# One store and one load per transpose, tiled products of two batches together, and a scheduler that models DMA: a four-layer graph network on one core

## Chip, cores and metric

The kernel runs on one core of one Trainium2 chip, in float32. The metric is device time in microseconds (us), the median of several executions. Engines are named as in the profile: PE (TensorE), DVE (VectorE), ACT (ScalarE), POOL (GpSimd), SP (SyncE, which issues DMAs). "A trip" is the way of a block through DRAM: store, load, transpose.

## The reference, cut to what matters

128 batches of 128 nodes with 512 features pass through four graph layers; each is `x = layernorm(x + layer(x, adj))`.

```python
# layer 0: H = sum_k Xk @ Wk[k] + bk[k], Xk = transition @ Xk (k = 0..2), transition from exp(leaky_relu(..)) * adj
# layer 1: two hypergraph convolutions, 512 -> 1024 -> 512, with relu and a layer norm between them
# layer 2: out = A @ x @ w, A from exp(lrelu(8 * tanh((s_i + s_j) / 8))) * adj
# layer 3: attention, 8 heads of 64; mask = adj + adj
q, k, v = proj(Wq, bq), proj(Wk, bk), proj(Wv, bv)
scores = einsum('bhqd,bhkd->bhqk', q, k) * SCALE * mask
ctx = einsum('bhqk,bhkd->bhqd', softmax(scores), v)
x = layernorm(x + ctx @ Wo.T + bo)
```

## The kernel before

Batches go in 64 pairs. The large products run as Strassen products (seven block products on PE, gathered from PSUM banks by DVE, ACT and POOL). All instructions of the whole program are first put in a list; a small simulation in the kernel file (`Plan.order`) then decides the order on every engine and which buffer each tile gets. **So an edit of one constant can move every instruction of the program.**

The left operands of the products have to be transposed. The kernel has DVE's transpose turn blocks of 32 x 32 (Q in the code) and leaves the moving of the blocks to a trip through DRAM: each of the four groups of 32 partitions is stored by its own DMA, one DMA loads the whole, DVE turns the blocks.

```python
def through_dram(src, name):
    _, nj, _, nw = src.shape
    d = scratch(name, 4, Q, 4, nj, nw)                    # Q = 32
    for j in range(nj):
        with plan.together():
            for m in range(4):
                sp.dma_start(part(d, lambda t, m=m, j=j: t.rearrange("k r m j w -> m j r k w")[m, j], j),
                             src[m * Q:(m + 1) * Q, j])
    def load():
        t = four()...                                     # cut: or sq() for the small ones
        sp.dma_start(t, part(d, lambda t: t.rearrange("k r m j w -> (k r) (m j w)"), 0, nj))
        return t
    return load

def turned(dst, t):
    ve.transpose(dst.rearrange("p q (m r) -> p m q r", r=Q), t.rearrange("p (m q a) -> p m q a", m=4, a=Q))

# layer 3, scores (cut; the product with v has the same form, one group per batch)
for b in range(U):                                        # U = 2 batches of a pair
    ps = [bank(), bank()]
    with plan.together(.6):
        for i in range(C):
            for r2 in range(2):
                pe.matmul(ps[r2][:, i * P:(i + 1) * P], qT[r2 * HD:(r2 + 1) * HD, b, i],
                          kT[r2 * HD:(r2 + 1) * HD, b, i], start=True, stop=True)
    # cut: DVE takes the banks into S, softmax, through_dram(S)
```

`four` is a tile of 128 x 1024 numbers (17 of them exist), `sq` one of 128 x 256, `bank` a PSUM bank (eight). The scheduler's estimate of a DMA was 60 ns of SP and 4500 ns until it has landed.

## Time and profile before

| | before |
|---|---|
| time, median of 3 runs | 5815.66 us (5813.88 to 5820.15) |
| busy: PE / DVE / POOL / ACT | 97% / 62% / 50% / 34% |
| transposes 128 x 1024 on DVE | 384, 1229 ns each |
| DMAs to store h, S and x3 for a trip | 4 per plane of 128 partitions |

The prediction below shows the busy shares, the windows and the timeline. Two more views matter later. First four lines of the page: groups of instructions (columns: busy us, mean ns of one, then idle time just before them and what ended it) and DMA issues (count, KB each, median us from issue to landing).

```profile
L307 PE MATMUL bank<-w,four 128*128 128x256 f32 (+1 forms) x14336 | 4044.3, 436 | 42.0 <-DVE four L307 31.1
...
L307 DVE STREAM_TRANSPOSE four<-four 128x1024 f32<-128x1024 f32 x384 | 467.5, 1229 | 75.3 <-DMA four<-x 31.0
...
h<-four SPq DMA_DIRECT2D x512, 128.0 KB, 2.4
four<-h SPq DMA_DIRECT2D x128, 512.0 KB, 3.9
```

And the largest wait of PE (who waits, for whom; then us in all, number of waits, longest):

```profile
PE bank L307 <- DVE four L307: 86.8, 63, 18.3
```

PE waits for DVE 63 times in the whole run. One of these waits, of 18.3 us, is that at the tail.

### The profile page before, as it was taken

Reading aid. Unit: us, or ns where it says so; the run is one execution under the profiler, and the core shown is the slowest. Engines: PE = TensorE matmul, PEld = TensorE weight load, DVE = VectorE, ACT = ScalarE, POOL = GpSimd, SP = SyncE. Lnnn points to the kernel's source line nnn. Section 1 sums busy time; section 2 is a strip of 40 time slices with the busy share of each in tenths; the row PEclk is TensorE's granted clock in tenths of the full one; section 3 lists DMA queues with packets and bytes.
Section 4 is the critical chain, followed back from the end, with each engine's and each line's share of the span. In section 5 each row is a group of like instructions: output and inputs, shape, how many; then the busy total and the mean of one; then the engine's idle time right before and its main releaser. Section 6 shows DMA issues by size and latency. Waiting matters only on the chain.

```text
span 5816.9 us, 87982 instructions
## 1 busy us (share of the span) xinstructions
PE 5665.4 (97%) x29077; PEld 4174.5 (72%) x29077; DVE 3591.1 (62%) x7654; ACT 1956.3 (34%) x5065; POOL 2895.7 (50%) x4553
## 2 busy tenths in 40 slices
PE   7999999999999999999999999999999999999997
PEld 4555555555666666666666688888888888888886
DVE  5656656665556555555555556666666666666664
ACT  1322222222333333333333333333333333333332
POOL 2333333332656666666666545555555555555553
PEclk9999999999999999999999999999999999999998
DMA  5433333332433344433333434444444444444443
GB/s 142 115 90 95 90 88 95 93 86 85 119 113 114 113 117 121 119 113 114 113 117 113 122 96 123 117 120 124 128 122 123 116 120 124 126 123 117 118 123 90
DMA packets 731128, 653.96 MB, mean 112 GB/s; under 512 B 270760, under 2 KB 584112, under 8 KB 730672
## 3 DMA queue, kind: packets, MB, share of 16 engines
q1 hardware_dynamic: 730672, 648.32, 38.7%
q8 instruction: 232, 3.80, 0.3%
q14 instruction: 224, 1.84, 0.1%
HBM read 362.81 MB, written 285.21 MB: 111 GB/s over the span
## 4 chain that ended last, share of the span: by engine, by line
PE 79%; DMA 8%; POOL 5%; DVE 3%; SPq 3%; issue 2%; ACT 1%; DVEq 0%; POOLq 0%; ACTq 0%
PE bank L307 79%; POOL four L307 3%; SPq L307 3%; DVE four L307 2%; DMA four<-x 2%; DMA four<-x1d 2%; POOL col L307 1%; ACT four L307 1%; DMA h<-four 1%; DMA four<-h 1%; DMA sq<-in_adj_dram 1%; DVE col L307 1%; DMA four<-in_x_dram 0%; DVE junk L307 0%; DMA four<-in_L_gnn_w_dram 0%
## 5 line engine op out<-in xcount | busy, mean ns | idle before, releaser
L307 PE MATMUL bank<-w,four 128*128 128x256 f32 (+1 forms) x14336 | 4044.3, 436 | 42.0 <-DVE four L307 31.1
L307 PEld LDWEIGHTS bank<-w,four 128*128 128x128 f32 x14336 | 2675.2, 191 | 1223.5 <-issue 789.7
L307 DVE TENSOR_TENSOR four<-bank,four 128x256 f32<-128x256 f32 (+1 forms) x1920 | 922.2, 483 | 1360.3 <-PE bank L307 1256.9
L307 ACT COPY four<-bank 128x256 f32<-128x256 f32 (+1 forms) x1280 | 571.4, 453 | 2173.2 <-PE bank L307 2160.3
L307 POOL TENSOR_TENSOR four<-four 128x256 f32<-128x256 f32 (+1 forms) x704 | 593.3, 855 | 1135.7 <-DVE col L307 620.4
L307 PE MATMUL bank<-four,w 128*128 128x128 f32 x7168 | 828.3, 276 | 31.6 <-DVE four L307 30.7
L307 PEld LDWEIGHTS bank<-four,w 128*128 128x128 f32 x7168 | 816.3, 193 | 47.2 <-issue 29.0
L307 POOL TENSOR_TENSOR four<-four,four 128x256 f32<-128x256 f32 (+1 forms) x832 | 708.5, 855 | 15.9 <-issue 1.4
L307 ACT ACTIVATE four<-four,col,col 128x512 f32<-128x512 f32 (+1 forms) x640 | 568.7, 897 | 438.1 <-POOL col L307 427.6
L307 POOL TENSOR_SCALAR col<-col 128x1 f32<-128x1 f32 (+1 forms) x704 | 213.3, 306 | 980.0 <-DVE col L307 946.5
L307 ACT ACTIVATE four<-four,col 128x128 f32<-128x128 f32 x1024 | 396.4, 393 | 679.1 <-DVE col L307 679.1
L307 DVE BATCH_NORM_STATS2 col<-four 128x6 f32<-128x512 f32 x768 | 523.2, 687 | 139.0 <-ACT four L307 128.0
L307 DVE STREAM_TRANSPOSE four<-four 128x1024 f32<-128x1024 f32 x384 | 467.5, 1229 | 75.3 <-DMA four<-x 31.0
L307 POOL TENSOR_TENSOR col<-col,neghalf 128x1 f32<-128x1 f32 x640 | 385.6, 605 | 22.9
L307 PE MATMUL bank<-four,sq 128*128 128x512 f32 x768 | 383.5, 594 | 10.2 <-ACT four L307 6.5
L307 PE MATMUL bank<-four,four 64*128 64x128 f32 (+1 forms) x4096 | 290.7, 284 | 21.2 <-DVE four L307 21.2
L307 PEld LDWEIGHTS bank<-four,four 64*128 64x128 f32 (+1 forms) x4096 | 235.4, 163 | 105.6 <-issue 43.7
L307 ACT ACTIVATE four<-four 128x512 f32<-128x512 f32 (+1 forms) x272 | 172.9, 636 | 347.9 <-DVE four L307 312.0
L307 POOL TENSOR_TENSOR four<-four,col 128x1024 f32<-128x1024 f32 x128 | 242.2, 1913 | 59.6 <-DVE col L307 59.6
L307 PEld LDWEIGHTS bank<-sq,four 128*128 128x128 f32 x2048 | 245.2, 193 | 29.3 <-issue 28.9
L307 PE MATMUL bank<-sq,four 128*128 128x128 f32 x2048 | 250.9, 276 | 0.0
L307 DVE SCALAR_TENSOR_TENSOR four<-bank,col,four 128x512 f32<-128x512 f32 x320 | 229.4, 730 | 22.3 <-PE bank L307 19.3
(77 smaller groups left out, 3419.5 us busy)
## 6 DMA issues: line engine op xcount, KB each, us to landing
h<-four SPq DMA_DIRECT2D x512, 128.0 KB, 2.4
four<-h SPq DMA_DIRECT2D x128, 512.0 KB, 3.9
S<-four SPq DMA_DIRECT2D x512, 128.0 KB, 2.5
four<-S SPq DMA_DIRECT2D x128, 512.0 KB, 4.3
four<-in_x_dram SPq DMA_DIRECT2D x64, 512.0 KB, 3.6
four<-in_x_dram SPq DMA_DIRECT2D x512, 64.0 KB, 2.1
x1d<-four SPq DMA_DIRECT2D x64, 512.0 KB, 2.9
four<-x1d SPq DMA_DIRECT2D x64, 512.0 KB, 5.5
```

Source lines behind the costliest of these rows:

```text
L307: call(*map(real, args), **{n: real(a) for n, a in kw.items()})
```

## The change

Its intent: fewer DMA issues, shorter trips, half as many changes of PE's tiling, and an order made with truer DMA times. The core of the diff (cut: bookkeeping of `run`, `parts` and DRAM tiles, deadlines, wider use of `ac.mul`):

```diff
-WHEN0 = (-3.0, -1.8, -.4, 0, .7)
+WHEN0 = (-1.5, -1.2, -.4, 0, .7)
-WHEN2 = (-2.4, -2.0, -1.35, -1.0, -.6, 0, .35, .7, .72, 1.2, 1.3, 1.31, 1.6)
-LAG1, LAG2 = 1, 1
+WHEN2 = (-2.4, -2.0, -1.35, -1.0, -.6, 0, .35, .7, 1.25, 1.6)
+LAG1, LAG2 = 1, 0.5
+RAMP = 0, 0, .2, 6
@@ LATENCY, row of SP
-           (4500, 4500, 4500, 4500, 4500))
+           (1400, 1400, 1400, 1400, 1400))
+ISSUE, BEGIN = 450, 1000
+EARLY = -0.5
@@ order: a DMA's transfer goes through one pipe; loads are gated by how far PE has come
+                if e == SP and ops[k][3][0] > reached and not ops[k][4]:
+                    continue
+            if o[7]:
+                end = pipe = max(pipe, t + BEGIN) + o[7]
@@ through_dram
-        d = scratch(name, 4, Q, 4, nj, nw)
+        d = scratch(name, 4, P, nj, nw)
         for j in range(nj):
-            with plan.together():
-                for m in range(4):
-                    sp.dma_start(... "k r m j w -> m j r k w" ..., src[m * Q:(m + 1) * Q, j])
+            sp.dma_start(part(d, lambda t, j=j: t.rearrange("k p j w -> j p k w")[j], j), src[:, j], run=nw)
-            sp.dma_start(t, ... "k r m j w -> (k r) (m j w)" ...)
+            sp.dma_start(t, ... "k (r m) j w -> (k r) (m j w)", m=4 ..., run=4 * nj * nw)
@@ turned
-    def turned(dst, t):
-        ve.transpose(dst.rearrange("p q (m r) -> p m q r", r=Q), t.rearrange("p (m q a) -> p m q a", m=4, a=Q))
+    def turned(dst, t, chunks=1):
+        src = t.rearrange("p (n a c) -> p n c a", a=Q, c=chunks) if chunks > 1 else t.rearrange(
+            "p (m q a) -> p m q a", m=4, a=Q)
+        ve.transpose(dst.rearrange("p q (r m) -> p m q r", r=Q), src)
@@ layer 3: one group for both batches (same for the product with v)
-        for b in range(U):
-            ps = [bank(), bank()]
-            with plan.together(.6):
+        ps = [[bank(), bank()] for _ in range(U)]
+        with plan.together(.65):
+            for b in range(U):
@@ prepare0: weights of the first products first, issued by ACT
+        load_blocks(WT["2"], wk0[2][:, :h], wk0[2][:, h:], True, ac.dma_start)
+        load_blocks(WT["10"], wk0[1], wk0[0], True, ac.dma_start)
```

`WHEN0` to `WHEN2` and `LAG1`, `LAG2` give every stage of a pair its place in the list, counted in pairs (the "key" of the prediction).

The price of the single store stands in `turned`. A row of the batch used to be numbered `32 m + r` (m the group of 32 partitions), so that what DVE wrote for one block was a run of 32 neighbouring numbers. Now it is `4 r + m`: neighbours in a block are written **four numbers, 16 bytes, apart**. For x, h and x3 the features are renumbered too, so that the transposes also read at 16 bytes (`c = 4`) or 32 bytes (`c = 8`, h).

> **What bounds the kernel now.** I read the page first (busy shares, the 40 slices), then a table of eight windows, then the waits of TensorE, then the timeline at the start, in steady layer 2/3 and at the tail.
>
> ```profile
> PE 5665.4 (97%) x29077; PEld 4174.5 (72%) x29077; DVE 3591.1 (62%) x7654; ACT 1956.3 (34%) x5065; POOL 2895.7 (50%) x4553
> ```
>
> TensorE (PE) is the bound: 97% busy, the next engine 62%. DMA engines are 38.7% busy. So only two things can move the time: PE instructions that become cheaper, and the 151 us in which PE has nothing to do. The windows (columns: length, then busy us and count of PE, PEld, DVE, ACT, POOL; granted clock, DMA share, GB/s) say where that idle time is:
>
> ```profile
> 0.00:60.00 60.00, 20.52 (x49) 12.19 (x50) 31.70 (x72) 6.04 (x15) 8.41 (x20) 0.91 0.83 217
> 290.00:1450.00 1160.00, 1160.00 (x3519) 657.23 (x3518) 696.85 (x1588) 284.99 (x685) 368.89 (x634) 1.00 0.32 91
> 1450.00:1750.00 300.00, 278.59 (x1065) 182.43 (x1064) 170.76 (x355) 112.81 (x191) 178.31 (x299) 0.98 0.39 116
> 1750.00:3200.00 1450.00, 1432.42 (x5465) 952.83 (x5465) 846.57 (x1728) 534.57 (x862) 894.72 (x1462) 1.00 0.40 115
> 3200.00:3500.00 300.00, 277.53 (x1603) 226.43 (x1602) 175.48 (x361) 97.86 (x256) 145.62 (x223) 0.97 0.37 108
> 3500.00:5670.00 2170.00, 2156.89 (x15870) 1915.66 (x15869) 1446.49 (x3081) 809.55 (x2740) 1163.09 (x1712) 1.00 0.42 122
> 5670.00:5817.00 147.00, 113.19 (x789) 96.67 (x787) 72.22 (x141) 44.26 (x161) 56.59 (x82) 0.88 0.31 92
> ```
>
> Idle PE: 39 us at the start, 21 and 22 at the two changes of layer, 34 at the tail; steady layer 0 has none, steady layer 1 18, steady layer 2/3 13. The starts of successive PE records show more than "busy" does, because a PE end is modelled. In clean stretches the step is 216 ns after a 256-column instruction, 429.5 after 512, 111.5 after 128, 109 after one with the identity, and on average 57 inside a tiled group (64 rows or 64 columns). Counts by these steps give a **floor of 5525 us**. The other 292 us are the pool from which any gain comes.
>
> Part of it is not idle at all. The attention products run as tiled groups of 16 instructions, one per batch:
>
> ```profile
> 4023.28 1.16 PE L307 MATMUL bank<-four,four 64*128 64x128 f32 x16
> 4024.38 1.99 PE L307 MATMUL bank<-w,four 128*128 128x256 f32 x8
> 4026.30 1.16 PE L307 MATMUL bank<-four,four 64*128 64x128 f32 x16
> 4027.39 1.13 PE L307 MATMUL bank<-w,four 128*128 128x256 f32 x4
> 4028.36 3.73 PE L307 MATMUL bank<-four,w 128*128 128x128 f32 x32
> ```
>
> From 4023.28 to 4028.36 are 5.08 us; the 12 full instructions are worth 12 x 0.216 = 2.59, the 32 tiled ones at 57 ns 1.82. The two groups cost 0.67 us beyond that, about **0.34 us per group**. In the records this is, in the median, 309 instead of 216 ns on the way in (+93), 201 instead of 57 on the way out (+144), and some 104 ns more on one step of the full product behind. 256 groups x 0.34 = 87 us. Of the 292, 205 us then remain as true waiting and half clock: start (to 290 us) 54, layer 0 nothing, first change of layer 29, layer 1 29, second change 31, layer 2/3 21, tail 41.
>
> The start, from the timeline, and the tail:
>
> ```profile
> 3.32 17.66 SPq L307 DMA_DIRECT2D w<-in_L_gnn_Wk_dram  x32
> 22.43 6.46 SPq L307 DMA_DIRECT2D four<-in_x_dram  x9
> 42.25 7.05 SPq L307 DMA_DIRECT2D four<-in_x_dram  x9
> 49.90 3.71 SPq L307 DMA_DIRECT2D e<-sq  x8
> ...
> 5795.21 1.98 PE L307 MATMUL bank<-four,four 128*64 128x128 f32 x16 [18.33 <-DVE four L307]
> ```
>
> SP needs about 0.45 us per DMA and issues 32 weight DMAs before the first row of x; the first store of e, ready at 39.6, queues behind prefetches for later pairs until 49.9. At the tail PE waits 18.3 us for the last softmax and its trip through DRAM.
>
> **What the Trainium skill says.** (1) "TensorEngine Tiling (Array Packing)", Key Properties: changing the tiling mode drains TensorE. The trace agrees, with the 0.34 us per group above. (2) "TensorE: Matmul & The Clock Gate", Part 1: after an idle window of about 3.4 us the array runs at half clock until it has been busy as long. The windows of 5 us agree: granted clock 0.50 at 50 to 55 us, behind a gap of 7 us, and again at 5795 to 5800. So each long gap removed also saves half of the next 3 us or so. (3) "DMA: Bandwidth & Descriptors", Issuing engines are not separate DMA queues: a second issuing engine saves only issue time. DMA share in the 5 us windows from 15 to 30 us is 1.00 to 1.06 at about 250 GB/s, so moving weight loads to ACT's queue removes the 17.7 us of SP but not the bytes. (4) "SBUF — State Buffer", Door 1: The DMA port swizzle: accesses that cross to a new 16-byte line each time pay a penalty. The changed DVE transposes write (and some read) at a stride of 16 bytes; the kernel before has none such, and its 1229 ns for 1024 columns are contiguous runs. No run so far shows what the stride costs.
>
> **The change part by part.**
>
> *Tiled products of both batches together.* 256 groups become 128 of 32 instructions. The instructions stay; 128 group overheads go: 128 x 0.34 = **-44 us**, nearly all in layer 2/3, directly on the bound. A check: at the tail the kernel before happens to run two score groups back to back as one x32 record of 2.06 us, against 1.16 each plus the overhead of two. It costs four PSUM banks at once instead of two, and the second batch's work comes later; I allow nothing for that.
>
> *One store per transpose.* For h, S, x3, e and F the stores fall from 512 to 128 each: 1920 DMA issues fewer, 1920 x 0.45 = 864 us of SP, which is idle half of the time. Its value is in latency: the x3 trip issues 8 stores (3.7 us), waits about 2, then loads; with 2 stores the load starts about 3 us sooner. In steady layer 2/3 PE loses 18 of its 21 us just ahead of the QK product (32 gaps of 0.57 us in the mean), which waits for this transpose. A chain shorter by 3 us removes most of them: **21 -> 9**. In layer 1 the 29 us are 105 stalls of 0.28 us between 512-column products, where DVE and POOL are late; the h trip is not what they wait for, so **29 -> 23**.
>
> *Start.* x and the weights of the first product come first, weights by ACT, later loads are gated. Bytes before the first product: 0.5 MB of x by blocks and 0.5 MB of weights, at about 250 GB/s and shared with the rest some 6 us; then the transpose (1.2 us): PE can start near 9 us instead of 36. It then has two "2" products of 6 us and the head of the "10" product, 5 us, to do. The "10" product needs 2 MB of weights, and e through DRAM: Wv dots until about 15 us as now, dots with x 3 us, exp and scaling 3, trip 6.5, so about 29 us. With the half clock at first I put the loss to 290 us at **54 -> 27**.
>
> *Changes of layer.* Truer DMA latencies (4.5 us flat before; the page shows 1.5 to 5.7) and layer 2/3 starting half a key earlier give the scheduler more to fill with, but the last weights can still load only when the layer 1 weights' buffer is free. **29 -> 19** and **31 -> 22**.
>
> *Tail.* The last pairs are pulled together by 0.2 key each. Behind the last scores there is still softmax (about 12 us for both batches), the trip (about 7), transposes, the last product and 8 us from there to the end; one product of 6 us of the pair before is all that fits in. **41 -> 33**.
>
> Removal of the ACT reordering copies and the merged weight loads concern setup only, under 5 us in all, and are inside these figures.
>
> Sum: 5525 floor + 44 for 128 groups + (27 + 0 + 19 + 23 + 22 + 9 + 33 = 133) = **5702 us**, 2.0% below 5815.66.
>
> **The rivals.**
> 1. *The waits move instead of going.* The order of all instructions is made anew. The scheduler might keep filling the same number of buffers, so that the changes of layer and the tail keep their loss, and only the group overhead and half of the start go: 5816 - 44 - 14 - 8 = about 5750. For: layer 1's stalls come from POOL and DVE, which the change leaves alone. Against: nearly every wait of the start is visibly a matter of DMA order.
> 2. *Strided transposes slow DVE.* If the 384 transposes of 1229 ns doubled, DVE would gain 467 us (62% -> 70%) and each round trip 1.2 us. PE would remain the bound; the gain from shorter chains in layers 1 and 2/3 would go: about 5720 to 5740.
> 3. *The schedule becomes nearly tight.* Layer 0 shows 1160 us without a single PE gap, so a good order is possible. If the steady layers reach that and the changes of layer fall below 12 us each: 5525 + 44 + 20 + 12 + 8 + 12 + 3 + 28 = about 5650.
> 4. *Four banks for scores starve the Strassen products* (three banks each, eight in all): the second group waits for DVE to empty banks. DVE's four 0.68 us operations per pair would put up to 1 us per pair on PE, 60 us, and take back the group gain. The x32 record at the tail speaks mildly against it.
>
> **Range and chances.** Group overhead is the surest term (44, give or take 10). The start is 54 -> 20 to 40, the rest together 151 -> 70 to 140. From that, low 5655 and high 5755. The border of 2% is 5815.66 / 1.02 = 5701.6, just under my figure, so it is close to even: faster 0.47, within 2% 0.51, slower 0.02 (nothing is added to PE).
>
> **What would show it.** Right: PE busy falls to about 5600 us with the same 29077 instructions; tiled records come as x32, about 128 of them; the first 256-column product starts before 12 us and PE idle to 60 us is below 25; SP issues 1920 DMAs fewer; the gap ahead of the QK product goes; the wait of 18 us at the tail shrinks by less than half. Wrong: transposes well over 1229 ns; new PE waits for DVE next to the scores; windows at the changes of layer with 20 us idle still; or, the other way, steady layer 1 without gaps, which would make the time less than 5670.

## The result

The changed kernel took **5897.59 us** (median of 4 runs, 5896.70 to 5898.48); the kernel before took 5817.90 us in the same rounds. The ratio is 1.0137 (95% interval 1.0120 to 1.0155): within 2%, but slower, and above the predicted range of 5655 to 5755. Ratios here are the mean time of one kernel's fast runs over that of the other's of the same rounds, so not quite the ratios of the medians quoted. Every run told of here was in the fast state. The kernel before was run again beside each call's experiments (medians 5813.69, 5829.94, 5814.99 and 5814.73 us).

From the page after:

```profile
PE 5682.4 (96%) x29077; PEld 4155.1 (70%) x29077; DVE 3937.4 (67%) x7654; ACT 1963.0 (33%) x5049; POOL 2927.2 (50%) x4553
...
L325 PE MATMUL bank<-w,four 128*128 128x256 f32 (+1 forms) x14336 | 4081.5, 436 | 162.4 <-DVE four L325 129.7
...
L325 DVE STREAM_TRANSPOSE four<-four 128x1024 f32<-128x1024 f32 x384 | 790.0, 2075 | 133.3 <-DMA four<-x 90.8
...
h<-four SPq DMA_DIRECT2D x128, 512.0 KB, 3.0
four<-h SPq DMA_DIRECT2D x128, 512.0 KB, 4.0
```

Number and mean time of PE's instructions are as before (29077; 436 ns), so nothing was added to PE. The idle time just ahead of its 256- and 512-column products grew from 42.0 to 162.4 us, 129.7 of it put down to DVE. On DVE it is the transposes that changed: the 384 large ones take 2075 instead of 1229 ns, 322.5 us more in all, and the 192 small ones 636 instead of 428 ns, another 40. PE's waits agree, more than three times as many as before:

```profile
PE bank L325 <- DVE four L325: 167.6, 227, 17.6
```

The windows after (length, then busy us and count of PE, PEld, DVE, ACT, POOL; clock, DMA share, GB/s), for the start, steady layer 0, 1 and 2/3, and the tail:

```profile
0.00:60.00 60.00, 35.20 (x106) 21.85 (x107) 34.52 (x72) 8.59 (x21) 14.07 (x25) 0.94 0.53 161
290.00:1480.00 1190.00, 1167.25 (x3503) 646.63 (x3502) 752.09 (x1584) 296.60 (x685) 402.11 (x638) 1.00 0.32 89
...
1780.00:3280.00 1500.00, 1455.43 (x5490) 953.54 (x5489) 968.05 (x1733) 529.20 (x867) 899.93 (x1479) 1.00 0.34 111
...
3580.00:5740.00 2160.00, 2105.68 (x15552) 1875.45 (x15551) 1531.62 (x3037) 805.49 (x2689) 1148.60 (x1690) 1.00 0.38 120
5740.00:5896.00 156.00, 131.45 (x968) 116.63 (x966) 93.24 (x161) 52.00 (x177) 61.73 (x94) 0.93 0.29 97
```

The tail gained, and the start at first: PE idle to 60 us is 25 us, not 39 (by 290 us that gain is gone again, see the table below). All three steady layers lost. Layer 0, which had no gap in 1160 us, now has 23 us of them in 1190; layer 1 has 45 instead of 18, layer 2/3 54 instead of 13. No DMA is near its limit there (0.32 to 0.38).

One such gap in steady layer 0, from the timeline after (start, duration, engine, operation, count of one kind in a row, idle before):

```profile
816.58 5.34 PE L325 MATMUL bank<-w,four 128*128 128x256 f32 x24
...
818.00 2.15 DVE L325 STREAM_TRANSPOSE four<-four 128x1024 f32<-128x1024 f32 x1
820.02 0.67 DVE L325 SCALAR_TENSOR_TENSOR junk<-four,wi_b 128x512 f32<-128x512 f32 x1
...
820.73 1.09 DVE L325 SCALAR_TENSOR_TENSOR junk<-four,wi_b 128x512 f32<-128x512 f32 x1
...
821.76 1.07 DVE L325 TENSOR_TENSOR four<-bank,four 128x256 f32<-128x256 f32 x3
822.55 1.13 PE L325 MATMUL bank<-w,four 128*128 128x256 f32 x4 [0.63 <-DVE four L325]
```

PE stops until DVE has done the second of three additions: they begin at 821.76, 822.09 and 822.43, and the second ends under 0.1 us before PE starts again. They take sums out of PSUM banks (`four<-bank,four`), so the likely reading is that PE lacks a free bank; the wait's own name is `bank <- DVE four`. The additions stand on DVE behind the transpose and two dot products of a **later** pair. DVE works in the order of its list (its 7654 instructions stand in the same order in the traces of this kernel and of c5, c9 and c10 below, whatever they wait for), so the transpose delays them; PE stands for 0.63 us.

### The profile page after: what moved, and what is told of

It reads as the page before. It is cut to its first block, busy times and chain, and to the rows that moved or that the text cites. A ratio compares the mean times of both kernels' runs of the same rounds, so it can differ in the third digit from the quotient of the medians.

```text
span 5895.8 us, 85595 instructions
## 1 busy us (share of the span) xinstructions
PE 5682.4 (96%) x29077; PEld 4155.1 (70%) x29077; DVE 3937.4 (67%) x7654; ACT 1963.0 (33%) x5049; POOL 2927.2 (50%) x4553
## 5 line engine op out<-in xcount | busy, mean ns | idle before, releaser
L325 PE MATMUL bank<-w,four 128*128 128x256 f32 (+1 forms) x14336 | 4081.5, 436 | 162.4 <-DVE four L325 129.7
L325 DVE TENSOR_TENSOR four<-bank,four 128x256 f32<-128x256 f32 (+1 forms) x1920 | 907.0, 481 | 1252.7 <-PE bank L325 1240.1
L325 DVE STREAM_TRANSPOSE four<-four 128x1024 f32<-128x1024 f32 x384 | 790.0, 2075 | 133.3 <-DMA four<-x 90.8
L325 PEld LDWEIGHTS bank<-four,w 128*128 128x128 f32 x7168 | 814.4, 192 | 18.3 <-issue 9.4
L325 POOL TENSOR_TENSOR col<-col,neghalf 128x1 f32<-128x1 f32 x640 | 431.9, 675 | 26.0
L325 ACT ACTIVATE four<-four 128x512 f32<-128x512 f32 x256 | 159.5, 625 | 527.3 <-DVE four L325 504.3
L325 PE MATMUL bank<-four,four 64*128 64x128 f32 (+1 forms) x4096 | 271.9, 280 | 26.1 <-DVE four L325 24.7
L325 POOL TENSOR_SCALAR sq<-sq,col 128x128 f32<-128x128 f32 x256 | 158.9, 631 | 190.9 <-DVE col L325 185.1
```

The source lines that it names most:

```text
L325: call(*map(real, args), **{n: real(a) for n, a in kw.items()})
```

## The experiments

Twelve kernels ran, in four calls. The main theory: the strided transposes cost DVE 0.85 us each, DVE is in order, and PE has no slack to make up for a late bank (T). The rivals: the new order itself, made with wrong estimates, is worse; the groups of both batches starve the Strassen products of banks; or the single store brings nothing that the others could be paid with.

### 1. Parts of the change, each with a new order

Four kernels first. **c1_four_stores** is the changed kernel with the old row order, so that DVE writes contiguous runs, at the price of four stores; features are still read at a stride.

```diff
+            with plan.together():
+                for m in range(4):
+                    sp.dma_start(... "k r m j w -> m j r k w" ..., src[m * Q:(m + 1) * Q, j], run=nw, parts=Q)
-        ve.transpose(dst.rearrange("p q (r m) -> p m q r", r=Q), src)
+        ve.transpose(dst.rearrange("p q (m r) -> p m q r", r=Q), src)
```

> The changed kernel with the old order of partitions in the trips through DRAM: four stores per plane again, and the DVE transposes write contiguous runs (the read stride of the feature order stays). Theory A (the strided write of the transposes, 2075 instead of 1229 ns, makes DVE late for TensorE): transposes back near 1230 ns, steady loss of TensorE in layer 0 from 36 us to under 8, time about 5720 us (5690 to 5760). Theory B (the new load timing, gating or DMA model starve TensorE): 5860 to 5900, layer 0 loss stays near 36. Theory C (products of both batches together): layers 0 and 1 keep their loss, 5860 to 5900.

Measured: 6101.29 us, ratio 1.0493 (1.0473 to 1.0512), correct. A miss: slower still. The groups by form explain part of it:

```profile
L325 DVE STREAM_TRANSPOSE four<-four 128x1024 f32<-128x1024 f32 x384 | 679.2, 1769 | 240.1 <-DMA four<-x 70.5 <-DMA four<-S 52.6 <-DMA four<-h 45.8
L325 DVE STREAM_TRANSPOSE sq<-sq 128x256 f32<-128x256 f32 x192 | 84.0, 437 | 53.0 <-DMA sq<-e 33.6 <-issue 11.2 <-DMA sq<-F 4.4
```

1769 ns is a mixture. In the trace each transpose that still reads at 16 or 32 bytes (x, h, x3) takes 2000 to 2150 ns; those of S, contiguous on both sides now, 1200 to 1250; the small ones went from 636 back to 437. So **a stride on the reading side alone costs as much as one on the writing side** (c2 and c6 below), **and both together hardly more** (2075 ns in the mean of the changed kernel, where two thirds have both). The rest of the loss comes from the stores and the new order, which this kernel can't separate.

**c2_before_one_store** is the kernel before with the single store and the strided write alone; no stride on the reading side, no change to the scheduler.

```diff
-            with plan.together():
-                for m in range(4):
-                    sp.dma_start(..., src[m * Q:(m + 1) * Q, j])
+            sp.dma_start(part(d, lambda t, j=j: t.rearrange("k p j w -> j p k w")[j], j), src[:, j])
-        ve.transpose(dst.rearrange("p q (m r) -> p m q r", r=Q), ...)
+        ve.transpose(dst.rearrange("p q (r m) -> p m q r", r=Q), ...)
```

> The kernel before with only the one store per plane and the transposes' strided write that comes with it; old scheduler model, timing and groups. Theory A: transposes near 2050 ns and slower than before, 5880 to 5960 us, since the old plan's start and tail stay. Theories B and C: within 1% of before, 5780 to 5840.

Measured: 5916.51 us, ratio 1.0176 (1.0161 to 1.0192), correct. Transposes 1966 to 2121 ns, DVE 3884.1 us busy. The single store with its stride is by itself a loss, without anything else of the change.

**c3_told** tells the scheduler of the changed kernel what a transpose now costs.

```diff
+        if name == "transpose":
+            return 160 + 1.87 * n
```

> The changed kernel with the scheduler told what the strided transposes take (160 + 1.87 ns per element instead of 67 + 1.04). Theory A1 (DVE has the room, the order is only planned with a wrong duration): most of the steady loss goes, 5720 to 5790 us. Theory A2 (the long transposes cost in themselves, whatever the order): 5860 to 5900. Theories B and C: no change, 5880 to 5900.

Measured: 5898.67 us, ratio 1.0148 (1.0131 to 1.0165): nothing gained over the changed kernel's 1.0137. The wrong estimate alone isn't the cause; this scheduler finds no better order when it knows the truth.

**c4_apart** puts the tiled products back into one group per batch, all else as changed.

```diff
-        with plan.together(.65):
-            for b in range(U):
+        for b in range(U):
+            with plan.together(.65):
```

> The changed kernel with one tiled group per batch again (256 groups of 16), all else kept. By the step of my prediction (0.34 us per group) it is 30 to 44 us slower than the changed kernel, 5925 to 5945 us. Theory C (together costs more than it saves): equal or faster, 5850 to 5900.

Measured: 6008.76 us, ratio 1.0337 (1.0321 to 1.0352): 111 us slower than the changed kernel. That is more than the edit can answer for, since layer 0, which has no such groups, also lost more (25 instead of some 10 us per 300 us, counted by PE's steps). In steady layer 2/3 the loss, changes of tiling included, was 23 instead of 18.3 us per 300 us, some 34 us over its 2160. Its trace has 214 stretches of tiled products against 125 in the changed kernel's; 89 x 0.34 us would be 30 us, an estimate that fits. This speaks against rival 4 of the prediction, but the new order blurs it; c5 below, with 4 us of idle PE in steady layer 2/3, settles it.

### 2. The same order, only the transposes changed

What was wanted was a kernel in which nothing else moves. The order depends on neither the stride nor its time, so turning the written layout back in `turned`, and nowhere else, leaves all instructions on all engines and all DMAs as they are. Rows then come out in a wrong order: **the result is wrong on purpose** (relative error 1.40 and 0.74), the work is the same.

**c5_after_contiguous**: the changed kernel, transposes contiguous on both sides.

```diff
-        src = t.rearrange("p (n a c) -> p n c a", a=Q, c=chunks) if chunks > 1 else t.rearrange(
-            "p (m q a) -> p m q a", m=4, a=Q)
-        ve.transpose(dst.rearrange("p q (r m) -> p m q r", r=Q), src)
+        ve.transpose(dst.rearrange("p q (m r) -> p m q r", r=Q), t.rearrange("p (m q a) -> p m q a", m=4, a=Q))
```

> The changed kernel, instruction for instruction in the same order on every engine, but each DVE transpose reads and writes contiguous runs (a wrong result on purpose). The first four runs showed that editing the program re-plans everything, and that a stride of 16 bytes on the read side alone also gives about 2050 ns; so here the plan is held fixed. Theory A (the stride is what cost): transposes 1230 ns, layer 0 without loss, 5690 to 5760 us, near my 5702. Theory B/C (the new plan, gating or groups): 5860 to 5900.

Measured: **5680.05 us** (5678.41 to 5682.61), ratio 0.9746 (0.9731 to 0.9761). 218 us less than the changed kernel by the medians, 227 by the ratios. The traces agree that nothing else moved: the sequence of instructions on PE, DVE, ACT and POOL is the same in both, one by one. The large transposes are back:

```profile
L325 DVE STREAM_TRANSPOSE four<-four 128x1024 f32<-128x1024 f32 x384 | 472.5, 1233 | 128.0 <-DMA four<-x 67.0
```

The same stretch of the timeline as above, in this kernel:

```profile
787.95 6.21 PE L325 MATMUL bank<-w,four 128*128 128x256 f32 x28
...
789.18 1.24 DVE L325 STREAM_TRANSPOSE four<-four 128x1024 f32<-128x1024 f32 x1
790.34 0.65 DVE L325 SCALAR_TENSOR_TENSOR junk<-four,wi_b 128x512 f32<-128x512 f32 x1
...
791.03 1.09 DVE L325 SCALAR_TENSOR_TENSOR junk<-four,wi_b 128x512 f32<-128x512 f32 x1
...
792.06 0.91 DVE L325 TENSOR_TENSOR four<-bank,four 128x256 f32<-128x256 f32 x2
```

The additions begin 2.88 us after the transpose's start, not 3.76, and PE's 28 instructions (24 and 4 above) run through without a gap. Over the whole run:

```profile
PE bank L325 <- DVE four L325: 56.8, 29, 18.0
```

227 waits have become 29. The windows of the steady layers (columns as before):

```profile
290.00:1330.00 1040.00, 1039.75 (x3153) 581.55 (x3152) 637.92 (x1432) 267.45 (x621) 366.76 (x573) 1.00 0.33 91
1630.00:3070.00 1440.00, 1432.50 (x5496) 957.67 (x5495) 880.25 (x1733) 528.84 (x876) 889.12 (x1462) 1.00 0.36 117
3370.00:5530.00 2160.00, 2156.19 (x16181) 1962.31 (x16180) 1458.86 (x3161) 844.82 (x2795) 1193.54 (x1758) 1.00 0.40 126
```

Idle PE: 0, 8 and 4 us. So the plan itself is good, and rival "worse order" falls.

One more rival can be checked in these traces, for steady layer 2/3: that the longer transposes cost through the longer trip, as the prediction's rival 2 had it, and not through DVE's queue. Count there the steps of full PE products that are over 0.15 us too long. Before, 29 of them, 17.8 us, stand ahead of the QK product, which waits for a trip. In the changed kernel one such gap is left (1.1 us), in c5 one (0.3 us). What the changed kernel has instead are 110 gaps of 0.55 us, 60 us, from one 256-column product to the next; c5 has 13 of them, 5.5 us. So PE hardly waits for a trip there in either, and the loss sits between products that wait for DVE's other work.

**c6_before_strided**: the kernel before, its transposes written at a stride of 16 bytes.

```diff
-        ve.transpose(dst.rearrange("p q (m r) -> p m q r", r=Q), ...)
+        ve.transpose(dst.rearrange("p q (r m) -> p m q r", r=Q), ...)
```

> The kernel before, same order on every engine, each DVE transpose writing at a stride of 16 bytes (wrong result on purpose). Theory A: transposes near 2050 ns, 384 of them, slower than before by 80 to 150 us, 5895 to 5965. If the old plan has slack enough: below 5850, and the slowdown of the changed kernel is a matter of its plan meeting the stride.

Measured: 6007.02 us (6003.79 to 6012.41), ratio 1.0308 (1.0291 to 1.0324), so 3.1% or 179 us for the stride alone in the old order. Here too the four engines' sequences are those of the kernel before, one by one. The results are wrong in c5 and in c6; one is faster and the other slower, so it isn't the wrong numbers that set the time.

```profile
L307 DVE STREAM_TRANSPOSE four<-four 128x1024 f32<-128x1024 f32 x384 | 770.3, 2032 | 63.4 <-DMA four<-x 24.8
PE bank L307 <- DVE four L307: 198.2, 192, 18.8
```

63 waits become 192. **T holds in both orders**, 179 us in the old, 218 to 227 in the new.

Two more kernels of this call kept the transposes contiguous and correct. **c7_old_layout** has the whole old layout (four stores, weights by blocks, reordering copies) under the new scheduler, times and groups:

```diff
-        d = scratch(name, 4, P, nj, nw)
+        d = scratch(name, 4, Q, 4, nj, nw)
+            with plan.together():
+                for m in range(4):
+                    sp.dma_start(..., src[m * Q:(m + 1) * Q, j], run=nw, parts=Q)
-        ve.transpose(dst.rearrange("p q (r m) -> p m q r", r=Q), src)
+        ve.transpose(dst.rearrange("p q (m r) -> p m q r", r=Q), t.rearrange("p (m q a) -> p m q a", m=4, a=Q))
```

> The changed kernel with the whole old layout (four stores per plane, weights by blocks with the reordering copies, all transposes contiguous), correct result, new scheduler model, gating, groups together, keys and ramp. Theory A: 5690 to 5780 us, since the model now has transposes right within 10%; the four stores at 0.45 us each are the only part of my prediction given up. If above 5850: the new model plans badly by itself (theory B).

Measured: 5945.67 us, ratio 1.0211 (1.0187 to 1.0236). A miss: DVE's transposes are fast, and it is slower than before and after. So contiguous transposes aren't enough; the new scheduler with four stores is bad for another reason. Part 3 takes that up.

**c8_before_together** has only the groups of both batches (and the ten stages that go with them) on the kernel before.

```diff
-WHEN2 = (-2.4, -2.0, -1.35, -1.0, -.6, 0, .35, .7, .72, 1.2, 1.3, 1.31, 1.6)
+WHEN2 = (-2.4, -2.0, -1.35, -1.0, -.6, 0, .35, .7, 1.25, 1.6)
-            with plan.together(.6):
+        with plan.together(.65):
+            for b in range(U):
```

> The kernel before with only the tiled products of both batches together (128 groups of 32) and the stage list that goes with it. By the step of my prediction: 30 to 50 us faster, 5765 to 5790. Theory C: same or slower, 5810 to 5860.

Measured: 5872.64 us, ratio 1.0074 (1.0057 to 1.0091). A miss. The changes of tiling did fall in its trace, from 252 stretches of tiled products to 67 (in 61 of them scores and the product with v stand back to back), but the new order brought a wait that wasn't there, for POOL:

```profile
PE bank L307 <- POOL four L307: 83.7, 117, 2.5
PE bank L307 <- DVE four L307: 84.6, 59, 18.6
```

Why the old scheduler came to place POOL's additions so late, no run settles. It shows again that one part of this change can't be priced by making it alone: the order comes out anew each time.

### 3. What one store is worth

**c9_plan_four** keeps the changed kernel's order on the compute engines to the letter. Each planned store is issued as four DMAs of 32 partitions in the old layout, the weights are reordered by their loads, the transposes are contiguous; the result is correct.

```diff
+        def dma_start(self, dst, src):
+            for m in range(4):
+                nc.sync.dma_start(dst[m], src[m * Q:(m + 1) * Q])
-            sp.dma_start(part(d, lambda t, j=j: t.rearrange("k p j w -> j p k w")[j], j), src[:, j], run=nw)
+            sp4.dma_start(part(d, lambda t, j=j: t.rearrange("k r m j w -> j m r k w")[j], j), src[:, j], run=nw)
```

> A correct kernel with the changed kernel's plan: the same order on the compute engines, but each planned store is issued as four DMAs of 32 partitions (the old layout), weights are reordered by their loads, and all transposes are contiguous. The plan counts each such store as one, so it does not know of the three further issues of 0.45 us. If the slow time of the run with four stores and the old layout, 5946 us, came from the plan that the scheduler makes when it counts them: near the 5680 us of the contiguous run, 5675 to 5760, and faster than both kernels. If four issues themselves hold TensorE up: 5800 to 5950.

**c10_two_stores** issues two DMAs of 64 partitions each. A row is then `64 h + 2 r + n`, so DVE writes at a stride of two numbers, 8 bytes.

```diff
-            for m in range(4):
-                nc.sync.dma_start(dst[m], src[m * Q:(m + 1) * Q])
+            for m in range(2):
+                nc.sync.dma_start(dst[m], src[m * 2 * Q:(m + 1) * 2 * Q])
+            ve.transpose(dst.rearrange("p q (h r n) -> p h n q r", h=2, n=2),
+                         t.rearrange("p (h n q a) -> p h n q a", h=2, n=2, a=Q))
```

> As the run before it, but each store is issued as two DMAs of 64 partitions, with the rows so interleaved that the transposes behind a trip through DRAM write at a stride of 8 bytes (loads of inputs stay contiguous). If two hits in a 16-byte line are enough: these transposes take about 1230 ns like the contiguous ones, and 5675 to 5740 us. If any stride costs the same: 320 of 384 transposes near 2050 ns and 5800 to 5880 us.

Measured: c9 6119.44 us, ratio 1.0527 (1.0510 to 1.0544); c10 5952.06 us, ratio 1.0239 (1.0221 to 1.0257); both correct. From c9's waits:

```profile
DVE four L325 <- DMA four<-x: 295.2, 63, 6.9
PE bank L325 <- DVE four L325: 284.7, 116, 15.5
```

From c10's page:

```profile
L325 DVE STREAM_TRANSPOSE four<-four 128x1024 f32<-128x1024 f32 x384 | 475.4, 1240 | 361.0 <-DMA four<-x 203.2
```

Two things follow. **A stride of 8 bytes on the writing side costs nothing**: 1240 ns against 1233 in c5 (320 of the 384 have it, and the longest of all takes 1264). And c9 takes 440 us more than c5 (6119.44 against 5680.05, the same sequence on the compute engines). Some 40 of them are lost before 290 us (81 against 41 by PE's steps), where c9's weights, which come in blocks, differ too; **in this plan the single store is worth about 400 us**. The wait has moved: DVE stands at the transpose of x3 until its load has landed, 295.2 us in c9 against 67.0 in c5, and since DVE is in order, PE's banks stay full behind it. Each of the four stores lands as fast as ever (2.4 us after its issue in the median, for h); but SP issues them 0.48 us apart, and the load can be issued only when the last has landed. The scheduler counts the landing from the start of a group as though it were one DMA, and leaves no time for it. That may answer c7 as well; no run shows it.

The waits themselves are not the whole loss. In c9, 47 of PE's steps are over 3 us too long, in c5 two, and the granted clock falls: 0.973 over the run, 0.996 in c5. Steps with no wait before them that took over one and a half times their usual length cost PE 138 us in c9 and 16 in c5; of the 138, 126 lie where the granted clock was 0.5. So over a quarter of the 440 us is PE at half clock.

**c11_two_told** is c10 with that mended: a planned store is 0.9 us of SP, its transfer begins after the second issue, and the load's shorter runs are counted. **c12_two_told_slack** allows 0.8 us more for each landing.

```diff
-        ns = estimate(engine, name, out, rest, kw) * self.share
+        ns = estimate(engine, name, out, rest, kw) * self.share * (issues if name == "dma_start" else 1)
-                end = pipe = max(pipe, t + BEGIN) + o[7]
+                end = pipe = max(pipe, t + max(o[2] - ISSUE, 0) + BEGIN) + o[7]
@@ c12 only, LATENCY of SP
-           (1400, 1400, 1400, 1400, 1400))
+           (2200, 2200, 2200, 2200, 2200))
```

> The run with two stores of 64 partitions and contiguous or 8-byte strides, planned anew with a scheduler that knows of the second issue, lets the transfer begin only after it, and knows the shorter runs of the load. Correct result. If the two-store run was slow (5952 us) because its plan did not know of the longer trips: 5690 to 5790 us, faster than both kernels. If plans with these trips are slow anyhow, as the one of the old layout was (5946): 5850 to 5960.

> As the run before it, with 0.8 us more allowed for each DMA's landing (2.2 instead of 1.4 us behind the modelled transfer), because the loads of h and S landed in 5.2 and 4.8 us in the two-store run against about 4 in the plan. If plans break where a transfer lands later than planned: faster than the run before it, 5680 to 5760. If the allowance only costs buffers: slower by 10 to 40 us.

Measured: c11 5872.23 us, ratio 1.0094 (1.0078 to 1.0111); c12 **5727.75 us** (5721.00 to 5733.10), ratio **0.9847** (0.9833 to 0.9862), both correct. c12 is faster than both kernels, by 1.5% and, by the ratios, 2.9%. Its waits:

```profile
PE bank L325 <- DVE four L325: 47.6, 27, 13.3
...
DVE four L325 <- DMA four<-x: 12.0, 16, 2.8
```

DVE's wait for x3 is 12.0 us instead of 203.2 in c10. The new order also has fewer changes of tiling (72 stretches of tiled products in the trace; 127 in c11). Of what c12's trace still has over c5's, some 50 us, 11 are lost by 290 us (its weights come by 32 DMAs on ACT's queue; 48 against 30 us in the first 60, in part made good), 13 at the change to layer 2/3 and 26 behind it.

A rival stands untested: the slack alone. The strided layout with the true time of a transpose (c3) and this slack gives no order at all; with the slack alone the changed kernel does build, but it was not timed, nor were four stores with it. So c12 is the fastest correct kernel here, and how much of its lead is the layout's is open.

## Why the prediction was wrong

The failed step is **the size in rival 2**. It named the mechanism rightly ("If the 384 transposes of 1229 ns doubled, DVE would gain 467 us (62% -> 70%)") and concluded "PE would remain the bound; ... about 5720 to 5740", that is 20 to 40 us over the main figure. The transposes rose by 0.85 us (69%), 357 us in all with the small ones (790.0 + 122.2 against 472.5 + 83.0 in c5), and 218 to 227 us of that, some six tenths, reached the end; in the old order 179 of 342. The main sum, 5702 us, had nothing at all for it. The step took DVE's busy share for its slack and charged the longer transpose to the trip alone, that is, to the gap ahead of the QK product. That gap did go, as predicted, in the changed kernel too; the loss came elsewhere (part 2). DVE is a queue in order that must empty PE's banks in time, with PE busy 97% of the span. As I read it, PE can't make up for a late bank, so a delay that is longer than the stock of free banks is lost for good; the waits fit this (29 in c5, 227 in the changed kernel), but no run changed the number of banks. The statement behind the chance of 0.02, "nothing is added to PE", is true and beside the point: what was added is PE's waiting.

The other terms can be held against c5, the changed plan without the stride, and against the changed kernel (loss in us, counted from the starts of PE's records in the way the prediction describes; rounded, so that the sums of c5 and of the changed kernel lie 3 to 4 us above their spans of 5678.6 and 5895.8):

| term | before | predicted | c5 | after |
|---|---|---|---|---|
| floor of PE's steps | 5525 | 5525 | 5525 | 5525 |
| tiled groups | 87 | 44 | 44 | 44 |
| start, to 290 us | 54 | 27 | 40 | 54 |
| layer 0 | 0 | 0 | 2 | 36 |
| first change of layer | 29 | 19 | 7 | 16 |
| layer 1 | 29 | 23 | 14 | 74 |
| second change | 31 | 22 | 14 | 24 |
| layer 2/3 | 21 | 9 | 9 | 96 |
| tail | 41 | 33 | 28 | 30 |
| sum | 5817 | 5702 | 5683 | 5899 |

- **Tiled groups.** Right. The groups are 128, a step into one takes 309 ns and out of one 201 to 203 ns in the median, as before. Rival 4 (starving banks) isn't seen in c5's layer 2/3.
- **Start.** Too hopeful by 13 us. The prediction had PE begin near 9 us. The first rows of x are eight DMAs, and issuing them alone takes SP 8 us; PE begins at 17.62. Between lies a wait for the rows to land: the first transpose starts only at 15.52. In c9, where the weights come as 32 small DMAs and not as four large ones, it starts at 7.76 and PE at 9.06; but PE then stands 7.75 us until the weights are there, and the first 60 us cost 47 us, against 31 in the changed kernel. So x and the weights seem to compete for the DMA engines; no run isolates it.

```profile
0.72 7.97 SPq L325 DMA_DIRECT2D four<-in_x_dram  x8
...
17.62 14.96 PE L325 MATMUL bank<-w,four 128*128 128x256 f32 x44 [17.62 <-DVE four L325]
```

- **One store.** The prediction gave it small values by layer (29 to 23, 21 to 9). In layer 2/3 c5 agrees (9), and for the reason given: the gap ahead of the QK product is gone. But the worth of a store depends on what the plan counts on: about 400 us in c9's comparison, since the order had been built on one. It isn't a saving over the kernel before, whose order had 4.5 us set aside for each landing.
- **Changes of layer and tail.** Rather better than predicted in c5 (7 and 14 against 19 and 22; 28 against 33). Rival 1, moved waits, didn't come. c5's 5680 lies between the main figure and rival 3.
- **The signs named as telling it wrong.** "Transposes well over 1229 ns" came true, and was the cause.

Open: why c8's order makes PE wait for POOL, how much of c4's 111 us is the groups' own, and what slack alone would do for the other layouts.

## What to carry to other kernels

On an engine that works in order and feeds the bound, its idle share is not its slack; what counts is for how long the bound can go on without it (here, by my reading, a few free PSUM banks). So price a longer instruction there by its added length times its count, of which a half to six tenths reached the end here, until a run says otherwise. A layout that saves DMAs must be checked on the stride that it leaves to the engines, in both directions: here 16 bytes cost 69% of a transpose and 8 bytes, tried on the writing side, nothing. Two stores with a stride of 8 bytes, and a scheduler told of both and given slack for the landing, made the fastest correct kernel; one store and four were not timed with that slack. And where a change makes the whole order anew, hold the order fixed and alter one duration, even at the price of a wrong result: of the experiments here only those gave clean differences (c9 and c10 hold the order too, but change the weights' loads with the stores).

## What the Trainium skill lacked or had wrong

- "SBUF — State Buffer", Specifications, row Cachelines: at least two hits per line of 16 bytes are needed for full bandwidth. The runs agree (8 bytes apart 1240 ns, 16 bytes apart 2075 ns, contiguous 1233 ns for 128 x 1024), but the page gives no size for the penalty on DVE: here its transpose takes 1.65 to 1.68 times as long, for read, write or both alike. Its note in Door 1 that one can stride for free up to "4 fp32" is easily read as allowing 16 bytes, which is just what cost it.
- "VectorE: DVE Perf Modes", The three transpose paths: no word on what a strided operand does to the transpose (432 to 636 ns for 128 x 256, 1233 to 2075 ns for 128 x 1024).
- "TensorEngine Tiling (Array Packing)", Key Properties: says that a change of mode drains TensorE, without a size. Here about 0.34 us per group of 64-row or 64-column products, of which 93 ns on the way in and 144 ns on the way out.
- No page that I read puts a price on splitting one store into several for a dependent load: here the parts are issued 0.48 us apart on SP, so that the last of four starts 1.4 us late, and four instead of one cost about 400 us in a plan made for one.
